# Moving where a one-core retention + feed-forward kernel rounds its weights, norms the next block and splits its output matrix

## The chip, the cores and the metric

The program runs on one core of one Trainium2 chip. The metric is the device time of one execution in microseconds (us), lower is better.

## The reference, cut to what matters

x has 4 sequences of 1024 tokens of width 512, in fp32. `LN` is a layer norm over the width without gain; lam is one decay for each of 16 heads.

```
h   = LN(x)
q, v = h @ Wq.T, h @ Wv.T                # 512 x 512 each
ret = scan over a sequence's tokens: state = lam * state + v_t
o   = LN(q * ret) * gamma + beta
o   = (o * silu(h @ Wg.T)) @ Wo.T
x   = x + LN(o)                           # "x1"
h   = LN(x)
g   = silu(h @ fp8(gate_w) * gate_scale)  # 512 x 1536, weights rounded to fp8 e4m3
u   = h @ fp8(up_w) * up_scale
d   = (g * u) @ fp8(down_w) * down_scale  # 1536 x 512
out = x + LN(d)
```

## The kernel before, in words

The 4096 tokens go through in 8 blocks of 512 (`NB = 8`), each with a retention part (class `Retention`) and a feed-forward part (class `Ffn`). The feed-forward part of block t runs in 12 steps (`for i in range(NI)`, one step for each 128 of the 1536 inner columns); between its products the order written out by hand places the retention part of block t+1, so that TensorE always has a product to run while the other engines do the element-wise work. In the loop `f` is the feed-forward part of block t, `b` is the retention part of block t+1, `n` that of block t+2 and `l` the feed-forward part before. Every engine takes its instructions in the order in which the program lists them (`InOrder`), so an instruction that waits holds up all that is listed behind it on its engine. SP issues nearly all transfers, in order too.

Ahead of the loop stands a long prologue. It runs block 0's retention part (`a`) with plain fp32 products, gets ready block 1's (`b`), and prepares weights for the whole run:

- **Roundings.** Gate, up and down weights come in 18 pieces of 1024 columns, in the order gate, up, down for each pair of steps (`pieces`). A piece is rounded by a VectorE cast to fp8 and a ScalarE activation back to fp32r (`round_weights`). One piece is three `yield`s, and `rounds(3)` runs one piece. Piece n is loaded into one of 7 buffers when an earlier piece has left it (`load_next`). Step i of block 0 needs the pieces of pair i//2; its down product runs two steps later (`lag = 2`).
- **Splits.** The q, v, g and o matrices are each split in four units into a top, a low and a scaled difference part (`Splitter.split`): three VectorE operations and one ScalarE activation. Units 0-3 are v, 4-7 q, 8-11 g, 12-15 o. `store` writes the parts to memory; later blocks stream them through a ring of four buffers (`w_ring`, `fetch_weights`). The units of o are loaded (`keep`), split and stored in block 1's steps; `Splitter.times` says when: `(block, step, place): "w12"` is a load, `s12` a split, `k12` a store, `r` new scratch room, `c12` a copy.
- **Block 1's x.** `b.stats`, `b.rstd`, `b.shift`, `b.norm_x` norm it (VectorE, GpSimd, ScalarE), `b.turn_x` transposes it on TensorE into banks pd0-pd3, `cut_x` takes the top part (VectorE, ScalarE) and the low part (VectorE), and `part_x` the difference. Then `b.begin(k, c)` runs the top and low passes of product k, unit c, ScalarE scales the bank, and `b.end(k, c)` adds the difference pass.
- **Block 1's norm of q * ret.** `halves` makes two fp32r halves of the sum (ScalarE, then VectorE), `mean` and `var` average them on TensorE, `center_y` subtracts and squares, `rstd_y` and `z` finish.

In step i of a block TensorE runs `f.gate(i)`, `f.up(i)` and `f.down(i - 2)`. Gate and up share two banks ("pf"): a gate product needs ScalarE's silu of the gate before (`gate<-pfg`), an up product needs VectorE's multiply of the up before (`gate<-pfu`). `fuse` then copies the result to fp32r on ScalarE and `rest` takes the remainder on VectorE. `scale(s)` takes the down sums from banks pd0-pd3 into `d`.

Down's weights in the kernel before lie in a changed order: of the 512 columns the even ones first and then the odd ones, written so by the rounding activation. `Ffn.down` reads them as `"p (k u) -> p u k"`, which gives the natural order in the bank. The same reading trick is used for fp32r products elsewhere; there the banks hold the two halves of a row in turns, and who reads such a bank does it through `in_order`.

Blocks 2-7 (`fast`) have no roundings, splits or prologue work.

Of the kernel before, what the change touches and what calls it, by code (L numbers as in the profile page):

```python
# [14 lines left out]
AF = mybir.ActivationFunctionType  # L15
ALU = mybir.AluOpType
# [7 lines left out]
def sandwich(  # L24
# [26 lines left out]
    NS = TB // P  # L51
# [15 lines left out]
    class InOrder:  # L67
# [42 lines left out]
    down_sb = wpool.tile([P, NI, D], F32R, tag="down_sb", name="down_sb")  # L110
    gate_v = gate_w.rearrange("(c p) f -> p c f", p=P)
    up_v = up_w.rearrange("(c p) f -> p c f", p=P)
    down_v = down_w.rearrange("(c p) f -> p c f", p=P)

    PW = 2 * NC * P
    pieces = []
    for h in range(NI // 2):
        pieces += [
            (gate_sb[:, :, ts(h, 2 * P)], gate_v[:, :, ts(h, 2 * P)]),
            (up_sb[:, :, ts(h, 2 * P)], up_v[:, :, ts(h, 2 * P)]),  # L120
            (
                down_sb[:, ts(h, 2), :].rearrange("p a (k u) -> p a u k", k=2),
                down_v[:, ts(h, 2), :],
            ),
        ]


# [10 lines left out]
    over = const.tile([P, len(pieces)], F32, tag="over", name="over")  # L138
# [28 lines left out]
    def as_dst(z, n):  # L167
        return z.rearrange("p (a b) -> p a b", a=2 if n % 3 == 2 else NC)

    def like(z, n):  # L170
        z = as_dst(z, n)
        return z.rearrange("p a (u k) -> p a u k", k=2) if n % 3 == 2 else z

    def load_piece(n):
        sp.dma_start(as_dst(parts[places[n]], n), pieces[n][1])

    def load_next(n):
        for m in range(n + 1, len(pieces)):
            if freed_by[m] == n:
                load_piece(m)  # L180

    def round_weights():


        for n in range(len(pieces)):
            w = parts[places[n]]
            if flag is None:
                yield
                act.copy(pieces[n][0], like(w, n))
                load_next(n)  # L190
                yield
            else:
                eighth = eighths[n % 2]
                dve.tensor_copy(eighth, w, saturate=False)
                load_next(n)
                yield
                act.activation(pieces[n][0], like(eighth, n), AF.Copy, accum_out=over[:, n : n + 1])
                yield
            yield

    rounding = round_weights()

    def rounds(n):
        for _ in range(n):
            next(rounding, None)
# [58 lines left out]
    def in_order(bank):  # L264

        return bank.rearrange("p (u k) -> p k u", k=2)
# [63 lines left out]
    class Splitter:  # L330
# [68 lines left out]
        def keep(self, n):  # L399
# [5 lines left out]

        times = {
            (0, 1, "end"): "c12", (0, 2, "end"): "c13", (0, 3, "end"): "c14", (0, 4, "end"): "c15",
            (1, 0, "mid"): "r w12 w13",
            (1, 0, "end"): "w14 w15", (1, 1, "end"): "s12", (1, 2, "start"): "s13",
            (1, 2, "end"): "k12 s14", (1, 3, "start"): "k13", (1, 3, "end"): "s15 k14",  # L410
            (1, 4, "mid"): "k15",
        }

        def at(self, *when):
# [491 lines left out]
    class Ffn:  # L906
# [60 lines left out]
        def scale(self, s):  # L967
            if s == 0:
                self.mv = small.tile([P, NS, 2], F32, tag="mv4", name=f"mvd_{self.t}", bufs=2)
            self.d[s] = work.tile([P, D], F32, tag="tok", name=f"d_{self.t}_{s}", bufs=4)  # L970
            dve.tensor_tensor(self.d[s], self.pds[s], ds_sb, ALU.mult)

        def stats(self, s):
            stats(self.d[s], self.mv[:, s, :])
# [49 lines left out]
    splitter = Splitter()  # L1024
    for n in range(8, 12):
        splitter.copy(n)
    b = Retention(1)
# [36 lines left out]
    a.scan(0)  # L1064
    a.v(1, "pf", later)
    a.scan(1)
    a.q(0)
    a.y_of(0)
    a.q(1)
    a.y_of(1)  # L1070
    splitter.split(8)
    a.v(2, "pf")
    a.scan(2)
    splitter.split(9)
# [2 lines left out]
    a.y_of(2)  # L1077
    splitter.split(10)
    splitter.store(9)
    b.stats(0)  # L1080
    a.v(3, "pf")
    a.scan(3)
    splitter.load("v")
# [2 lines left out]
    for n in range(4, 8):  # L1086
        splitter.copy(n)
    splitter.store(10)
    for s in range(1, NS):
        b.stats(s)  # L1090
    a.q(3)
    splitter.load("q")
    for n in range(4, 7):
        load_piece(n)
    a.y_of(3)
    b.rstd()
    b.shift()
    splitter.split(11)
    rounds(2)
    a.g_of(0, "pf")  # L1100
    for s in range(NS):
        b.norm_x(s, True)
    a.mean()
    a.center_y()
    splitter.store(11)
    b.new_xnT()
    a.g_of(1, "pf")
    b.turn_x(0, "pd0")
    b.turn_x(1, "pd1")
    b.cut_x(0)  # L1110
    b.cut_x(1)
    a.gate(2, "pf")
    b.turn_x(2, "pd2")
    b.turn_x(3, "pd3")
    b.cut_x(2)
    b.cut_x(3)
    splitter.split(0)
    rounds(3)
    a.silu(2)
    a.gate(3, "pf")  # L1120
    a.silu(3)
    splitter.store(0)
    a.var()
    for s in range(NS):
        b.part_x(s)
    a.rstd_y()
    for c, home in enumerate(("pa0", "pf", "pf", "pa1")):
        b.begin("g", c, home)
    for c in range(NC):
        a.z(c)  # L1130
    for c in range(NC):
        b.end("g", c)
    splitter.split(1)
# [1 line left out]
    a.o(0, "pd0")  # L1135
    splitter.split(2)
    splitter.store(1)
    rounds(3)
    a.o_moments(0)
    a.x1_of(0)  # L1140
    a.o(1, "pd1")
    splitter.split(3)
    splitter.store(2)
# [1 line left out]
    a.x1_moments(0)  # L1145
    a.x1_of(1)
    a.x1n_of(0)
    a.o(2, "pd2")
    rounds(1)
    a.o_moments(2)  # L1150
    a.x1_moments(1)
    a.x1_of(2)
    a.x1n_of(1)
    splitter.store(3)
    a.o(3, "pd3")
    splitter.split(4)
    a.new_x1nT()
    b.begin("v", 0, "pf")
    a.turn_x1n(0)
# [23 lines left out]
    splitter.store(5)  # L1183
    b.begin("q", 0, "pd2")
    b.end("v", 3)
    rounds(3)
    b.begin("q", 1, "pd3")
    a.turn_x1n(3)
    a.upper_of(3)
# [1 line left out]
    splitter.split(7)  # L1191
    splitter.store(6)
    a.rest_of(3)
    rounds(3)
    b.begin("q", 2, "pf")
    b.end("q", 1)
    b.begin("q", 3, "pf")
    rounds(3)
    b.end("q", 2)
    rounds(3)  # L1200
    b.end("q", 3)
    splitter.store(7)

    l = None
    for t in range(NB):
        f, n = Ffn(a), None
        fast = b is not None and b.fast
        for i in range(NI):
            if t > 0 and (t > 1 or i) and not (fast and i == 11):
                (f if i else l).rest((i - 1) % NI)  # L1210
            if t == 0 and i == 0:
                n = Retention(2)

            if t > 0 and b and i == 0 and t < NB - 2:
                n = Retention(t + 2)
# [23 lines left out]
            if t == 0 and 7 <= i < 11:  # L1239
                b.x1_moments(i - 7)  # L1240
            f.gate(i)
            if t == 0 and i in (4, 5):
                n.norm_x(2 * i - 8, True)
                n.norm_x(2 * i - 7, True)
            if fast and i < 7:
                b.gap(3 * i)
            if fast and 7 <= i < 10:
                b.o_gap(3 * i - 21)
            if t == 0 and i == 6:
                n.fetch_x()  # L1250
            splitter.at(t, i, "start")
            if n and t and i == 2:
# [27 lines left out]
            if t == 0 and i == 4:  # L1280
# [3 lines left out]
                b.z(3)  # L1284
            if t == 0 and 6 <= i < 10:
                b.o(i - 6)
            if t == 0 and i == 7:
                b.new_x1nT()
            if t == 0 and 7 <= i < 10:
                b.x1n_of(i - 7)  # L1290
# [81 lines left out]
            if n and t and i == 8:  # L1372
                n.low_of(2)
                n.low_of(3)
            if t == 0 and i in (7, 8):
                n.low_of(2 * i - 14)
                n.low_of(2 * i - 13)
            if t == 0 and i == 10:
                n.diff_of(0)
                n.diff_of(1)  # L1380
# [5 lines left out]
                    n.diff_of(2)  # L1386
                    n.diff_of(3)
            if t == 0:
                if i == 0:
                    rounds(3)  # L1390
                    b.halves()
                    rounds(3)
# [16 lines left out]
            if n and i == (6 if t else 5):  # L1409
                n.new_xnT()  # L1410
            if t == 0 and 6 <= i < 10:
                b.x1_of(i - 6)
# [72 lines left out]
        l, a, b = f, b, n  # L1485
# [116 lines left out]
```

## Time and profile before

| | |
|---|---|
| time, median of 3 runs (range) | 924.46 us (923.93 to 926.37) |
| the profiled execution | 924.62 us, its span 922.8 us |
| TensorE busy, instructions | 888.1 us (96%), 3948 |
| VectorE, ScalarE, GpSimd busy | 629.1 us, 424.7 us, 239.8 us |
| mean granted TensorE clock | 0.992 |

The span is from the first to the last instruction; the other 1.8 us of the profiled execution lie around it. In the profile every instruction of the kernel has line L75 (the helper `InOrder`), so groups are told apart by the names of their tiles: `pfg` and `pfu` are the banks of gate and up, `pd` of down, `pv`, `pq`, `pg` of the retention products, `ptx` of block 1's turned x, `mu` and `var` the averages, `scr` a buffer of raw weights, `split_room` the splits' scratch, `wo_parts` the split o. In a timeline the columns are start, duration, engine, operation, tiles and count; a bracket gives the idle time before it and what released it.

### The profile page before, as it was taken

How to read it: one execution, taken by the hardware profiler on the slowest of the kernel's cores; microseconds unless marked ns; L12 is line 12 of the kernel's file. 1: busy time of each engine (PE TensorE's matmuls, PEld its weight loads, DVE VectorE, ACT ScalarE, POOL GpSimd, SP SyncE). 2: the span in 40 equal slices, each digit the busy share in tenths (PEclk: the TensorE clock that was granted, in tenths of full speed). 3: DMA queues.
4: the chain of work that ended last, by engine and by line, in shares of the span. 5: the costliest groups of instructions: out<-in, count | busy, mean ns of one | idle time of the engine just before them, and what ended most of it. 6: DMA issues, size and time to landing. Idle time of an engine off the chain costs nothing. (4 is left out here: it accounts for less than half of the span.)

```text
span 922.8 us, 11982 instructions
## 1 busy us (share of the span) xinstructions
PE 888.1 (96%) x3948; PEld 742.6 (80%) x3948; DVE 629.1 (68%) x1071; ACT 424.7 (46%) x741; POOL 239.8 (26%) x304
## 2 busy tenths in 40 slices
PE   9999869999799999999999999999999999999995
PEld 7465657787688888888888888888888888888885
DVE  4878677658568775876758766686758755665545
ACT  1277666433354435553364534644364533644323
POOL 1214220311322314141232304232141502422030
PEclk9999999999899999999999999999999999999999
DMA  9963654557445666727745467537656365434021
GB/s 285 307 195 130 186 187 119 142 160 261 151 141 123 192 217 195 189 61 254 237 128 150 158 203 240 155 88 240 211 170 178 104 217 151 133 105 114 1 93 49
DMA packets 115579, 152.69 MB, mean 165 GB/s; under 512 B 10867, under 2 KB 54644, under 8 KB 115444
## 3 DMA queue, kind: packets, MB, share of 16 engines
q1 hardware_dynamic: 114644, 151.18, 53.3%
q10 hardware_dynamic: 864, 0.66, 0.3%
q8 instruction: 33, 0.54, 0.3%
q14 instruction: 38, 0.31, 0.1%
HBM read 117.46 MB, written 38.54 MB: 169 GB/s over the span
## 5 line engine op out<-in xcount | busy, mean ns | idle before, releaser
L75 PE MATMUL pfg<-x1nT,gate_sb 128*128 128x512 f32 x768 | 184.4, 383 | 2.1 <-ACT gate L75 1.9
L75 PE MATMUL pfu<-x1nT,up_sb 128*128 128x512 f32 x768 | 184.4, 383 | 0.7 <-DVE gate L75 0.7
L75 PE MATMUL pd<-down_sb,fuse 128*128 128x512 f32 x720 | 170.5, 379 | 0.0
L75 PEld LDWEIGHTS pfg<-x1nT,gate_sb 128*128 128x128 f32 x768 | 145.1, 190 | 26.0 <-ACT gate L75 5.1
L75 PEld LDWEIGHTS pfu<-x1nT,up_sb 128*128 128x128 f32 x768 | 146.1, 190 | 23.7 <-issue 1.4
L75 PEld LDWEIGHTS pd<-down_sb,fuse 128*128 128x128 f32 x720 | 141.3, 196 | 14.6
L75 DVE SCALAR_TENSOR_TENSOR gate<-pfu,us_sb,gate 128x512 f32<-128x512 f32 x96 | 71.8, 748 | 71.8 <-PE pfu L75 61.2
L75 ACT CAST fuse<-gate 128x512 fp32r<-128x512 f32 x90 | 55.6, 618 | 134.2 <-DVE gate L75 134.0
L75 ACT ACTIVATE gate<-pfg,gs_sb 128x512 f32<-128x512 f32 x96 | 65.7, 684 | 94.3 <-PE pfg L75 94.3
L75 POOL TENSOR_SCALAR mv<-mv 128x1 f32<-128x1 f32 (+1 forms) x82 | 22.2, 271 | 319.7 <-DVE mv L75 317.7
L75 DVE TENSOR_TENSOR fuse<-gate,fuse 128x512 fp32r<-128x512 f32 x90 | 70.5, 783 | 6.1 <-ACT fuse L75 6.1
L75 POOL TENSOR_TENSOR d<-d,x 128x512 f32<-128x512 f32 x28 | 41.7, 1511 | 86.0 <-ACT d L75 72.1
L75 DVE BATCH_NORM_STATS2 st<-x 128x6 f32<-128x512 f32 x64 | 43.5, 680 | 20.1 <-POOL x L75 17.3
L75 POOL TENSOR_TENSOR mv<-mv,nhalf 128x1 f32<-128x1 f32 (+1 forms) x75 | 52.7, 702 | 6.2
L75 POOL TENSOR_TENSOR x<-x,x1n 128x512 f32<-128x512 f32 x32 | 45.5, 1429 | 18.8 <-ACT x1n L75 11.8
L75 ACT ACTIVATE pv<-pv 128x512 f32<-128x512 f32 x28 | 16.3, 582 | 54.1 <-PE pv L75 54.1
L75 POOL TENSOR_TENSOR ysum<-y 128x512 f32<-128x512 f32 x8 | 10.8, 1347 | 108.6 <-DVE y L75 108.6
L75 POOL TENSOR_TENSOR sqsum<-sqsum,sq 128x512 f32<-128x512 f32 x24 | 33.4, 1390 | 17.3 <-ACT sq L75 15.5
L75 DVE TENSOR_TENSOR y<-pq,y 128x512 f32<-128x512 f32 x28 | 19.1, 681 | 23.0 <-PE pq L75 23.0
L75 DVE SCALAR_TENSOR_TENSOR y<-y,lnb_sb,mids 128x512 f32<-128x512 f32 x28 | 27.0, 965 | 7.1 <-ACT mids L75 7.0
L75 ACT ACT_TABLE_LOAD x19 | 24.4, 1283 | 16.0 <-DVE var L75 11.5
L75 DVE BATCH_NORM_STATS2 st<-po 128x6 f32<-128x512 f32 x32 | 21.9, 684 | 14.1 <-PE po L75 14.1
(214 smaller groups left out, 1494.0 us busy)
## 6 DMA issues: line engine op xcount, KB each, us to landing
x<-in_x SPq DMA_DIRECT2D x52, 256.0 KB, 5.2
kept<-x SPq DMA_DIRECT2D x32, 256.0 KB, 3.1
x<-kept SPq DMA_DIRECT2D x32, 256.0 KB, 4.2
out<-d SPq DMA_DIRECT2D x31, 256.0 KB, 2.0
w_ring<-dtop_v SPq DMA_DIRECT2D x24, 256.0 KB, 3.2
w_ring<-dlow_v SPq DMA_DIRECT2D x24, 256.0 KB, 3.7
w_ring<-ddiff_v SPq DMA_DIRECT2D x24, 256.0 KB, 3.7
w_ring<-dtop_q SPq DMA_DIRECT2D x24, 256.0 KB, 2.7
```

The costliest lines, as they stand in the source:

```text
L75: return lambda *args, **kwargs: tc.keep_in_program_order(op(*args, **kwargs))
```

## The change: what it does

Down's weights are rounded in their natural order, and `scale` reads the down banks through `in_order` instead. In the prologue block 1's `stats`, `norm_x`, `turn_x` and `cut_x` move from behind block 0's v, q products to between them; `silu(3)` moves behind `var` and `rstd_y`. The roundings of the prologue are spread anew (8 pieces before the loop as before), and in block 0's steps one piece is rounded in each of steps 0-5 and two in each of steps 6 and 7, where it was two in each of steps 0-4. Block 1's first `halves` moves to step 1 and its `mean` and `center_y` behind step 1's up product; its second `halves` goes before the roundings of step 2. Block 2's x is normed, sent, fetched and parted one step later in block 0 (stats in steps 0-3). Block 1's units of o are all loaded at the start of block 1's step 0, split in step 0 (two) and step 3 (two).

```diff
-            (
-                down_sb[:, ts(h, 2), :].rearrange("p a (k u) -> p a u k", k=2),
-                down_v[:, ts(h, 2), :],
-            ),
+            (down_sb[:, ts(h, 2), :], down_v[:, ts(h, 2), :]),
...
-                act.activation(pieces[n][0], like(eighth, n), AF.Copy, accum_out=over[:, n : n + 1])
+                act.activation(pieces[n][0], as_dst(eighth, n), AF.Copy, accum_out=over[:, n : n + 1])
...
-            (1, 0, "mid"): "r w12 w13",
-            (1, 0, "end"): "w14 w15", (1, 1, "end"): "s12", (1, 2, "start"): "s13",
-            (1, 2, "end"): "k12 s14", (1, 3, "start"): "k13", (1, 3, "end"): "s15 k14",
-            (1, 4, "mid"): "k15",
+            (1, 0, "start"): "r w12 w13 w14 w15", (1, 0, "mid"): "s12", (1, 0, "end"): "s13",
+            (1, 1, "start"): "k12", (1, 1, "mid"): "k13", (1, 3, "start"): "s14",
+            (1, 3, "end"): "s15", (1, 4, "start"): "k14", (1, 4, "end"): "k15",
...
-            dve.tensor_tensor(self.d[s], self.pds[s], ds_sb, ALU.mult)
+            halves = "p (k u) -> p k u"
+            dve.tensor_tensor(
+                self.d[s].rearrange(halves, k=2), in_order(self.pds[s]), ds_sb.rearrange(halves, k=2),
+                ALU.mult,
+            )
...
     a.scan(1)
+    b.stats(0)
     a.q(0)
     a.y_of(0)
+    b.stats(1)
+    b.stats(2)
     a.q(1)
     a.y_of(1)
+    b.stats(3)
+    b.rstd()
+    b.shift()
     splitter.split(8)
+    for s in range(NS):
+        b.norm_x(s, True)
     a.v(2, "pf")
...
-    b.stats(0)
+    b.new_xnT()
+    b.turn_x(0, "pd0")
+    b.turn_x(1, "pd1")
     a.v(3, "pf")
...
-    for s in range(1, NS):
-        b.stats(s)
+    b.turn_x(2, "pd2")
+    b.turn_x(3, "pd3")
+    b.cut_x(0)
     a.q(3)
...
-    b.rstd()
-    b.shift()
     splitter.split(11)
-    rounds(2)
+    b.cut_x(1)
     a.g_of(0, "pf")
-    for s in range(NS):
-        b.norm_x(s, True)
     a.mean()
     a.center_y()
     splitter.store(11)
-    b.new_xnT()
     a.g_of(1, "pf")
-    b.turn_x(0, "pd0")
-    b.turn_x(1, "pd1")
-    b.cut_x(0)
-    b.cut_x(1)
-    a.gate(2, "pf")
-    b.turn_x(2, "pd2")
-    b.turn_x(3, "pd3")
     b.cut_x(2)
     b.cut_x(3)
+    rounds(3)
+    a.g_of(2, "pf")
     splitter.split(0)
-    rounds(3)
-    a.silu(2)
     a.gate(3, "pf")
-    a.silu(3)
-    splitter.store(0)
     a.var()
     for s in range(NS):
         b.part_x(s)
     a.rstd_y()
+    a.silu(3)
+    splitter.store(0)
...
     for c in range(NC):
         a.z(c)
+    rounds(3)
     for c in range(NC):
         b.end("g", c)
...
     splitter.store(1)
-    rounds(3)
     a.o_moments(0)
     a.x1_of(0)
+    rounds(2)
     a.o(1, "pd1")
...
+    rounds(1)
     a.o(2, "pd2")
-    rounds(1)
+    rounds(3)
+    splitter.split(4)
     a.o_moments(2)
...
-            if t == 0 and i in (4, 5):
-                n.norm_x(2 * i - 8, True)
-                n.norm_x(2 * i - 7, True)
+            if t == 0 and i in (5, 6):
+                n.norm_x(2 * i - 10, True)
+                n.norm_x(2 * i - 9, True)
...
-            if t == 0 and i == 6:
+            if t == 0 and i == 7:
                 n.fetch_x()
...
             if t == 0 and i == 1:
-                b.mean()
-                b.center_y()
-            if t == 0 and i == 2:
-                n.stats(2)
-                n.stats(3)
-                n.rstd()
-                n.shift()
+                b.halves()
...
             f.fuse(i)
+            if t == 0 and i == 1:
+                b.mean()
+                b.center_y()
+            if t == 0 and i == 2:
+                b.halves()
...
-            if t == 0 and i in (7, 8):
-                n.low_of(2 * i - 14)
-                n.low_of(2 * i - 13)
+            if t == 0 and i in (8, 9):
+                n.low_of(2 * i - 16)
+                n.low_of(2 * i - 15)
...
             if t == 0:
-                if i == 0:
-                    rounds(3)
-                    b.halves()
-                    rounds(3)
-                elif i == 2:
-                    rounds(5)
-                    b.halves()
-                    rounds(1)
-                elif i < 6:
-                    rounds(6)
+                rounds(3 if i < 6 else 6 if i < 8 else 0)
                 if i < 11:
                     f.rest(i)
-                if i < 2:
+                if i < 4:
                     n.stats(i)
+                if i == 3:
+                    n.rstd()
+                    n.shift()
...
-            if t == 0 and i in (4, 5):
-                n.send_x(2 * i - 8)
-                n.send_x(2 * i - 7)
+            if t == 0 and i in (5, 6):
+                n.send_x(2 * i - 10)
+                n.send_x(2 * i - 9)
```

More of the change, by code (lines that the diff above doesn't have):

```diff
@@ L168, in as_dst @@
         return z.rearrange("p (a b) -> p a b", a=2 if n % 3 == 2 else NC)
-    def like(z, n):
-        z = as_dst(z, n)
-        return z.rearrange("p a (u k) -> p a u k", k=2) if n % 3 == 2 else z
     def load_piece(n):
@@ L188, in round_weights @@
                 yield
-                act.copy(pieces[n][0], like(w, n))
+                act.copy(pieces[n][0], as_dst(w, n))
                 load_next(n)
@@ L1155, in sandwich @@
     a.o(3, "pd3")
-    splitter.split(4)
     a.new_x1nT()
@@ L1193, in sandwich @@
     a.rest_of(3)
-    rounds(3)
     b.begin("q", 2, "pf")
     b.end("q", 1)
+    rounds(3)
     b.begin("q", 3, "pf")
-    rounds(3)
     b.end("q", 2)
@@ L1202, in sandwich @@
     splitter.store(7)
+    rounds(3)
     l = None
@@ L1286, in sandwich @@
                 b.o(i - 6)
-            if t == 0 and i == 7:
+            if t == 0 and i == 8:
                 b.new_x1nT()
@@ L1388, in sandwich @@
             if t == 0:
-                if i == 0:
-                    rounds(3)
-                    b.halves()
-                    rounds(3)
-                elif i == 2:
-                    rounds(5)
-                    b.halves()
-                    rounds(1)
-                elif i < 6:
-                    rounds(6)
+                rounds(3 if i < 6 else 6 if i < 8 else 0)
                 if i < 11:
                     f.rest(i)
-                if i < 2:
+                if i < 4:
                     n.stats(i)
+                if i == 3:
+                    n.rstd()
+                    n.shift()
             if l and not b and i in (4, 5):
@@ L1408, in sandwich @@
                     l.rstd()
-            if n and i == (6 if t else 5):
+            if n and i == 6:
                 n.new_xnT()
```

## The prediction

> **What bounds the kernel now.** I read the page first, then a table by stages, then TensorE's (PE's) timeline and the queues of ScalarE (ACT) and VectorE (DVE) around its gaps.
>
> ```profile
> span 922.8 us, 11982 instructions
> PE 888.1 (96%) x3948; PEld 742.6 (80%) x3948; DVE 629.1 (68%) x1071; ACT 424.7 (46%) x741; POOL 239.8 (26%) x304
> ```
> ```profile
> 109.00:150.00 41.00, 32.05 (x132) 25.53 (x132) 29.74 (x47) 29.60 (x44) 9.39 (x9) 0.96 0.51 172
> 232.00:262.00 30.00, 24.70 (x95) 20.12 (x96) 16.59 (x25) 11.72 (x21) 10.82 (x11) 0.89 0.46 149
> 300.00:900.00 600.00, 598.45 (x2776) 522.03 (x2775) 405.02 (x687) 269.31 (x471) 164.98 (x203) 1.00 0.53 161
> ```
>
> The columns of the stages are length, PE, weight loads, DVE, ACT, GpSimd (POOL), granted clock, DMA share, GB/s. From 300 to 900 us PE is busy 99.7% at clock 1.00: no reordering gains there, and the change leaves the products as they are. What can go lies before 262 us, where the same table (rows not shown) leaves PE idle 23.6 us. Its waits, with what a wait costs behind it:
>
> ```profile
> 106.85 1.99 PE L75 MATMUL pq<-up_sb,slot 128*128 128x512 f32 x8 [1.92 <-ACT pq L75]
> 116.55 0.49 PE L75 MATMUL mu<-half,mean_r 128*128 128x512 f32 x1 [2.26 <-ACT half L75]
> 127.37 1.99 PE L75 MATMUL pfg<-x1nT,gate_sb 128*128 128x512 f32 x8 [1.33 <-ACT gate L75]
> 132.84 0.50 PE L75 MATMUL var<-half,mean_r 128*128 128x512 f32 x1 [3.48 <-ACT half L75]
> 134.16 3.13 PE L75 MATMUL pfu<-x1nT,up_sb 128*128 128x512 f32 x8
> 232.70 2.07 PE L75 MATMUL pq<-diff,w_ring 128*128 128x512 f32 x4 [4.14 <-ACT pq L75]
> 248.07 0.49 PE L75 MATMUL mu<-half,mean_r 128*128 128x512 f32 x1 [3.31 <-ACT half L75]
> 249.13 3.45 PE L75 MATMUL pfg<-x1nT,gate_sb 128*128 128x512 f32 x8
> ```
>
> Eight fp32r matmuls take 1.73 us start to start elsewhere. After the three gaps over 3 us the next ones take 1.0 to 1.6 us more (clock 0.91 there); after 2.26 us they do not. The releasers are ACT and, behind them, DVE: queues with too much listed ahead of a short operation.
>
> ```profile
> 114.06 1.96 ACT L75 ACTIVATE down_sb<-scr 128x1024 fp32r<-128x1024 fp8e4 x1
> 115.89 0.60 ACT L75 CAST half<-ysum 128x512 fp32r<-128x512 f32 x1
> 117.86 1.06 ACT L75 ACTIVATE gate_sb<-scr 128x1024 fp32r<-128x1024 fp8e4 x1 [1.36 <-DVE scr L75]
> ```
>
> A down piece takes 2.0 us, a gate piece 1.06: the difference is down's changed order.
>
> I follow the new queues by hand with these durations: DVE cast, add or subtract 0.6-0.7, split 1.85, stats with aggregate 0.85; ACT gate, copy or scale 0.5-0.6, piece 1.25 with its accumulator read. Times are in the frame of before's timeline.
>
> **Down's order.** Six down pieces go from 2.04 to 1.06 us on ACT, 6 us in all, counted below only where PE waits. The price is a bank read at every second element in `scale`, 32 times, four of them in the tail where PE is done.
>
> ```profile
> L75 DVE TENSOR_TENSOR y<-pq,y 128x512 f32<-128x512 f32 x8 | 5.4, 680 | 5.4 <-PE pq L75 5.4
> L75 DVE TENSOR_TENSOR d<-pd,ds_sb 128x512 f32<-128x512 f32 x4 | 2.5, 677 | 0.0
> ```
>
> `y<-pq,y` already reads in this stride and takes 680 ns against 677 for the straight read: price nothing. The Trainium skill, page "SBUF — State Buffer", section "SBUF: two separate sides", speaks against the change: it puts PSUM in 8-byte lines and calls any non-contiguous access there significantly slower, at least for matmuls. Taken as a doubling, an estimate of mine, it would put the four reads in the tail and so the end 2.7 us later. The row shows no such price on DVE and decides.
>
> **Prologue to 68 us.** Block 1's x has all landed (at most 5.4 us after issue at 14.3) before its stats run. Four stats end at 26.2, GpSimd's chain (2.63 us, as at 41.55-44.18) behind its sum at 29.4, the norms on ACT (4 x 0.73) have the second x at 31.1; PE reaches the turn at 31.3. So the 1.11 us wait at 47.20 and its slow restart (0.3) go. New: silu(3) now stands behind the Sqrt load (var turned 56.3, loads 2 x 1.28, root 0.32, silu 0.6), ends at 59.8 and holds the bank that PE wants at 59.2: 0.75 in place of 0.25. o starts at 67.0 instead of 68.1: **1.1**. Bounds: 1.7 with no new wait; -0.9 if DVE's split is held up twice more, because a GpSimd operation beside its subtract makes it 1.64 instead of 0.69 us (as at 25.69).
>
> **To the loop, 68 to 109 us.** DVE goes without a break from the scan of v0 to split 6, 10.6 us (87.40-98.03), and still does: split 5, split 6, three scans. It starts 1.2 earlier, so PE's wait for q0's scale grows from 0.41 to 1.7 while the 0.91 before goes. The last q waits 1.2 instead of 1.92 (a down piece ahead of it on ACT, 1 us shorter). gate(0) starts at 106.5 instead of 108.83: **1.2** more. Bounds -1 and 3.2 (all three waits).
>
> **Steps 0-5 of block 0.** Before: gate(0) at 108.83, gate(6) at 150.24, 41.4 us. PE's work there is 16 x 1.73 for gates, ups and downs, 1.3 for mu and var, 28.9 in all; the rest is waits, slow clock and restarts. New waits: mu: gate(1)'s silu behind one piece (111.55 + 1.25) ends at 113.5, its halves at 114.1 and 114.9 while PE is there at 113.5: 1.5. gate(3): the squares, one piece and gate(2)'s silu end at 121.75, 0.85 late. var 0.6 in all, gates 4 and 5 about 0.2. With 5 restarts of 0.2: 28.9 + 3.15 + 1.0 = 33.1, so **8.3**. Block 2's first stats now stand ahead of half and multiply on DVE and wait for x issued at 108.3; I have it landed by 113, before it costs. Landing 8 us after issue (the slowest issues of the first 70 us) would cost 2.8. Bounds 4 and 12.5 (all waits).
>
> **Steps 6-11 of block 0.** Two pieces per step in 6 and 7 put 2.5 us on ACT ahead of block 1's o chain (stats, GpSimd, ACT, GpSimd add, stats, transpose), and block 2's `low_of` (2.2 us on DVE) moves to steps 8 and 9. Before PE never waited here; fuse(8) and fuse(9) now come 2-5 us late, covered by the o product (3.4) and down (1.7) between; fuse(10) comes at 181.5 with PE there at 180.6. Price **-1.0**, bounds 0 and -4.
>
> **Block 1.** Before, splits 13 and 14 stood in steps 2 and 3 ahead of multiplies that PE waited for.
>
> ```profile
> 227.66 1.64 DVE L75 TENSOR_TENSOR wo_parts<-wo_parts,split_room 128x512 fp32r<-128x512 f32 x1
> 230.77 0.74 DVE L75 SCALAR_TENSOR_TENSOR gate<-pfu,us_sb,gate 128x512 f32<-128x512 f32 x1
> 240.93 0.43 DVE L75 TENSOR_SCALAR split_room<-wo_parts 128x512 int32<-128x512 int32 x1 [4.54 <-DMA ddiff_o<-split_room]
> ```
>
> The last line is split 14 waiting for split 12's store, which now comes two steps earlier: that stall goes, and with it most of mu's wait; split 14 then costs 1.85 ahead of step 3's multiply, and mu's halves come 0.7 after PE. But splits 12 and 13 now stand ahead of the scans of v2 and v3 and wait for their loads: SP issues four from 203.5 on, DVE is there at 205.3 and goes on at 207.5 to 209. The scan of v3 then ends at 218.6-220, PE needs its bank at 218.9; the scale of q2 ends at 229.8-231.2 while PE is there at 228.4-229.8. And the ring's next load stands behind four more issues of 0.45 us. So 4.14 + 1.6 (slow clock) become 1.5 + 1.0: gain 3.2. At mu 3.31 becomes 0.7, gain 2.8 with the second half's 0.23; the slow clock behind it (1.6) goes too, but var then waits that much longer, for its chain hangs on mu: nothing. Together **6.0**, bounds 2 and 8.5.
>
> **Sum.** 1.1 + 1.2 + 8.3 - 1.0 + 6.0 = 15.6. The profiled execution took 924.62 (span 922.8 and 1.8 around it), 0.2 from the median: **909.0 us**. The ends of the terms will not all fall together; 905 to 913 for this case.
>
> **The rivals.**
> - *Given back* (917): the chain of block 1's o does not fit a step of 8.65 us; each of steps 8-11 loses 1.5 and block 1's scans start late. For it: fuse(8) some 5 us late by my own walk. Against: DVE was 64% busy from 150 to 200. 913 to 921.8.
> - *Everything goes* (900): the queues have more slack than my in-order walk gives, and 23.6 us of idle plus 4 of slow clock mostly vanish. Against: the two chains above are DVE-bound by rows. 896 to 905.
> - *Slower* (930): DVE becomes the bound from step 6 of block 0 to step 3 of block 1. Each of steps 6-11 takes 1.5-2 longer (10), the scans of v2 and v3 come 5 later behind two splits that wait for their loads, the halves and multiplies behind them as well, so the gaps over 3 us are back with their slow clock (11). It decides once a chain step takes over 11.5 us where 8.65 are to be had. Against: DVE's idle rows between 155 and 190 are waits of 1 to 3 us for PE and GpSimd, not a full queue.
> - *Nothing* (924): the waits only move by as much.
>
> **How the numbers follow.** This kernel can tell 0.3% (2.8 us) from no change. Chances: forecast 0.55, given back 0.19, everything 0.14, nothing 0.04, slower 0.08. Faster 0.88, same 0.04, slower 0.08. The range leaves out slower (0.08), nothing (0.04), the part of everything below 899 (0.04) and of given back above 920 (0.03): 899 to 920.
>
> **What would show it.** Right: down pieces at 1.06 us on ACT; no wait at the turn of block 1's x; gate(6) of block 0 near 139.5; waits for mu and var under 2 us in both blocks and no clock under 1.00 from 109 to 232; `d<-pd` still near 0.68 us. Wrong: PE waiting for `gate` or `x1nT` in steps 8-11, for `w_ring` or a scan in block 1's steps 0-2, or `st<-x` on DVE held by a DMA in step 0.

## The result, and the profile after

The changed kernel takes 912.7 us (median of 4 runs, 911.73 to 913.68) against 924.19 for the kernel before (4 runs, 923.03 to 926.37). The ratio is 0.9873, 95% interval 0.9851 to 0.9894: 11.7 us less (the medians differ by 11.5). The forecast was 909.0, 15.6 us less. The profiled execution took 913.0 us, its span is 911.2, and it is set against the profiled execution of before, 924.62 and 922.8.

The head of the page, and two stages (stretch, PE, weight loads, DVE, ACT, POOL, granted clock, DMA share, GB/s):

```profile
span 911.2 us, 11999 instructions
PE 884.0 (97%) x3948; PEld 741.0 (81%) x3948; DVE 631.3 (69%) x1071; ACT 419.0 (46%) x741; POOL 241.4 (26%) x304
```
```profile
109.00:150.00 41.00, 38.19 (x158) 30.43 (x157) 32.76 (x52) 25.33 (x42) 8.12 (x9) 0.96 0.49 166
150.00:200.00 50.00, 47.59 (x198) 36.98 (x197) 30.64 (x55) 22.55 (x46) 12.29 (x18) 1.00 0.59 171
```

From 109 to 150 us PE went from 32.05 to 38.19 us busy (158 matmuls instead of 132, for the changed kernel is further along by then), at the same mean clock of 0.96. From 150 to 200, where it never waited before, PE now stands idle 2.4 us. ACT lost 5.7 us of work in all: six down pieces shortened by 1.0 us. PE's timeline of the changed kernel shows which waits went and which came:

```profile
104.72 1.13 PE L75 MATMUL pq<-up_sb,slot 128*128 128x512 f32 x4 [0.81 <-ACT pq L75]
113.09 0.49 PE L75 MATMUL mu<-half,mean_r 128*128 128x512 f32 x1 [0.31 <-ACT half L75]
115.57 0.79 PE L75 MATMUL mu<-half,mean_r 128*128 128x512 f32 x1 [1.99 <-DVE half L75]
116.16 3.07 PE L75 MATMUL pfg<-x1nT,gate_sb 128*128 128x512 f32 x8
181.19 1.99 PE L75 MATMUL pfg<-x1nT,gate_sb 128*128 128x512 f32 x8 [1.53 <-ACT gate L75]
184.06 2.00 PE L75 MATMUL pfu<-x1nT,up_sb 128*128 128x512 f32 x8 [0.88 <-DVE gate L75]
204.14 1.13 PE L75 MATMUL pv<-low,w_ring 128*128 128x512 f32 x4 [2.10 <-DMA w_ring<-dlow_v]
214.02 1.13 PE L75 MATMUL pq<-diff,w_ring 128*128 128x512 f32 x4 [0.98 <-ACT pq L75]
248.19 1.52 PE L75 MATMUL var<-half,mean_r 128*128 128x512 f32 x2 [2.54 <-ACT half L75]
251.21 2.12 PE L75 MATMUL pfg<-x1nT,gate_sb 128*128 128x512 f32 x8
```

The four big waits of before (1.92 for the last q, 2.26 for mu, 3.48 for var, 4.14 for q2) are 0.81, 0.31, 0.29 and 0.47; block 1's mu is 0.90 in place of 3.31. New are DVE's half at 115.57, gate(11)'s wait for the silu of gate(10) at 181.19, the ring's load at 204.14, and a longer wait for block 1's var at 248.19 (0.83 before).

All runs are compared below by the starts of the same four products on PE: gate(0) and gate(6) of block 0, gate(0) and gate(7) of block 1. The columns are the lengths of the stretches between them, taken from each kernel's PE timeline.

| kernel | to gate(0) | steps 0-5 | steps 6-11 | block 1 to gate(7) | rest of the span |
|---|---|---|---|---|---|
| before | 108.83 | 41.41 | 49.67 | 77.16 | 645.7 |
| changed | 105.69 | 34.17 | 52.52 | 74.62 | 644.2 |
| e1 down alone | 107.88 | 40.02 | 49.57 | 77.53 | 646.0 |
| e2 prologue alone | 106.28 | 41.13 | 49.67 | 78.36 | 645.8 |
| e3 steps alone | 108.94 | 35.15 | 54.22 | 77.50 | 646.1 |
| e4 o's splits alone | 109.08 | 42.64 | 49.67 | 75.61 | 646.0 |
| f1 loads later | 105.70 | 33.01 | 52.52 | 75.07 | 647.1 |
| f2 stats later | 106.24 | 32.93 | 52.52 | 74.53 | 645.9 |
| f3 roundings earlier | 105.93 | 33.14 | 50.70 | 73.22 | 645.8 |
| f4 split 15 later | 105.51 | 34.90 | 52.51 | 70.72 | 646.7 |
| g1 old down order | 106.61 | 33.87 | 54.79 | 75.62 | 647.0 |
| g2 three edits | 106.00 | 32.92 | 51.08 | 70.10 | 646.4 |
| g3 five edits | 105.35 | 32.91 | 50.62 | 72.13 | 645.3 |
| h1 five and the loads | 106.10 | 32.94 | 50.75 | 72.29 | 647.2 |

One trace is one execution: e4's steps 0-5 have the instructions of before and took 1.2 us longer, at a clock of 0.89. The last column lies after all that the change moves, apart from the strided reads, and varies by 3 us among these kernels. So the 1.5 us that the changed kernel's trace has over before there are scatter, and only differences that a wait or a clock explains are read from single stretches. Across chips the ratios are compared.

### The profile page after: what moved, and what is told of

Its sections match the earlier page's. It is cut to its first block, busy times and chain, and to the rows that moved or that the text cites. A ratio compares the mean times of both kernels' runs of the same rounds, so it can differ in the third digit from the quotient of the medians.

```text
span 911.2 us, 11999 instructions
## 1 busy us (share of the span) xinstructions
PE 884.0 (97%) x3948; PEld 741.0 (81%) x3948; DVE 631.3 (69%) x1071; ACT 419.0 (46%) x741; POOL 241.4 (26%) x304
## 4 chain that ended last, share of the span: by engine, by line
PE 85%; DVE 7%; ACT 3%; DMA 2%; issue 1%; POOL 1%; DVEq 0%; SPq 0%; ACTq 0%; POOLq 0%
PE pfu L75 17%; PE pfg L75 16%; PE pd L75 15%; PE pg L75 9%; PE po L75 9%; PE pv L75 9%; PE pq L75 8%; DVE st L75 1%; DVE y L75 1%; PE idle L75 1%; DVE gate L75 1%; DMA x<-in_x 1%; PE var L75 1%; PE mu L75 1%; PE pt L75 1%
```

## The experiments

**The parts alone.** Each kernel is the kernel before with one part of the change, as the diff above has it.

*e1, down's order alone:*

```diff
-            (
-                down_sb[:, ts(h, 2), :].rearrange("p a (k u) -> p a u k", k=2),
-                down_v[:, ts(h, 2), :],
-            ),
+            (down_sb[:, ts(h, 2), :], down_v[:, ts(h, 2), :]),
```

> The kernel before with down's weights in natural order alone: six rounding pieces fall from 2.04 to 1.06 us on ACT, scale reads its bank in stride. My theory (the parts add, and a shorter piece counts only where PE waits behind it): of the pieces before the loop and in steps 0-4, those ahead of pq (1.92 at 106.85), mu (2.26 at 116.55) and var (3.48 at 132.84) matter, some 1 us each for two or three of them: 1 to 3 us less than before, about 922.5. Rival A (all in the ACT queue's length): the whole gain of the change comes from the shorter pieces, 6 us or more gone, 918 or less. Rival B (the strided reads cost): 32 reads dearer than 0.68 us, the same time as before or more, and the tail after 900 us longer.

Measured: ratio 0.9976 (0.9966 to 0.9987), 923.59 us against 925.02. The gain lies where a long piece stood ahead of PE: the last q's wait fell from 1.92 to 1.03, mu's from 2.26 to 1.49; var's rose from 3.48 to 4.32 and took some of it back. The reads of the down banks, first of before, then of the changed kernel (the tile's rows: count, min/median/max in ns, first and last start):

```profile
L75 DVE TENSOR_TENSOR d<-pd,ds_sb x32: 670/679/692, 224.2 to 914.2; 128x512 f32<-128x512 f32 x32
```
```profile
L75 DVE TENSOR_TENSOR d<-pd,ds_sb x32: 670/679/692, 218.8 to 902.5; 128x512 f32<-128x512 f32 x32
```

The strided read costs nothing (680 ns in e1), so rival B falls. So does rival A: 2.2 us, not 6. The theory's 1 to 3 us hold.

*e2, the prologue's order alone:* (the hunks from `a.scan(1)` to the loop)

```diff
+    b.new_xnT()
+    b.turn_x(0, "pd0")
+    b.turn_x(1, "pd1")
     a.v(3, "pf")
```

> The kernel before with the new order ahead of the loop alone (block 1's x normed and parted among block 0's products, the prologue's roundings spread anew; down still in the changed order, the loop as it was). Theory: the wait of 1.11 us at 47.20 and the slow restart go and gate(0) comes 2 to 3 us earlier than 108.83 (3.14 in the kernel after, some of it from shorter down pieces); nothing in the loop can take it back, since its queues start as much earlier: 921.5 to 922.5 in all. Rival (the wait moves): the wait for the ACT pieces ahead of the last q product grows by as much and gate(0) starts within 1 us of 108.83: 923.5 to 924.5.

Measured: ratio 0.9973 (0.9963 to 0.9983), 922.56 us. gate(0) starts at 106.28, 2.55 us earlier; the last q still waits 1.69. The theory's numbers hold.

*e3, block 0's steps alone:*

```diff
-                if i == 0:
-                    rounds(3)
-                    b.halves()
-                    rounds(3)
...
-                elif i < 6:
-                    rounds(6)
+                rounds(3 if i < 6 else 6 if i < 8 else 0)
```

> The kernel before with the new spread of roundings, halves, mean and block 2's x in block 0's steps alone (one piece in each of steps 0-5, two in 6 and 7; the prologue as it was; down pieces still 2.04 us). Theory: this is the largest term of the change: gate(0) to gate(6) took 41.4 us before and 34.2 after, so gate(6) comes some 5 to 7 us earlier, of which steps 6 to 11 give back 3 as they did in the kernel after (2.85): 3 to 4 us less in the end, about 920.5. Rival (the spread needs the short down pieces and the early prologue): pieces of 2.04 us in steps 2 and 5 hold silu and halves, gate(6) gains under 3 us and steps 6 to 11 give it all back: 923.5 or more.

Measured: ratio 0.9984 (0.9971 to 0.9996), 923.68 us. Steps 0-5 gain 6.3 us, as the theory said; then steps 6-11 give back 4.55, more than the 3 expected, and 1.5 us are left. What gave it back, in e3:

```profile
187.13 1.99 PE L75 MATMUL pfg<-x1nT,gate_sb 128*128 128x512 f32 x8 [2.43 <-ACT gate L75]
190.00 1.99 PE L75 MATMUL pfu<-x1nT,up_sb 128*128 128x512 f32 x8 [0.87 <-DVE gate L75]
```

So the theory had the gain of steps 0-5 right and the loss behind it too small. The rival, 923.5 or more, allows a gain of 0.7 us at most on the 924.19 above, and it looked for the loss in the wrong place (silu and halves in steps 2 and 5). The 1.5 us (0.4 to 2.7 by the interval) lie between the two.

*e4, o's splits alone:* (the table `times` of the change)

> The kernel before with o's splits in steps 0 and 3 of block 1 alone. Theory: the wait of 4.14 us at 232.70 and of 3.31 at 248.07 with their slow restarts (1.6 each) shrink, as in the kernel after, where block 1's steps 0-5 still held 2.10 for w_ring and 2.54 for var: gain 2.5 to 4, about 921. In the trace w_ring is waited for about 2 us behind the four loads of o. Rival (the splits' place does not matter, the wait only moves from step 2 to step 0 and from mu to var): within 1 us of before, 923.5 to 924.5.

Measured: ratio 0.9971 (0.996 to 0.9982), 922.57 us. Block 1's stretch gains 1.5 us in the trace and the runs 2.7: the q2 and mu waits shrank from 4.14 and 3.31 to 0.31 and 0.90, while 2.42 for dlow_v came and var rose to 2.54. The theory's lower end.

The four ratios add to 0.96% (8.9 us of 925); the whole change gives 1.27%, 2.9 us more. In the traces the parts fall short in two stretches: in steps 6-11, where alone they sum to -4.45 and the change has -2.85, and in block 1, where alone they sum to -0.36 and the change has 2.54. In block 1 part of it is the slow clock behind a wait: the gate behind the ring's late load took 2.76 us in e4 and 1.89 in the changed kernel, and the step with the wait of 4.14 us for q2 took 17.35 us in e2 and 16.20 before. This may be scatter; no run settles it. For steps 6-11 g1 below puts the question.

**The waits that were left.** Each kernel is the changed kernel with one edit.

*f1, two of o's loads later:*

```diff
-            (1, 0, "start"): "r w12 w13 w14 w15", (1, 0, "mid"): "s12", (1, 0, "end"): "s13",
-            (1, 1, "start"): "k12", (1, 1, "mid"): "k13", (1, 3, "start"): "s14",
+            (1, 0, "start"): "r w12 w13", (1, 0, "mid"): "s12", (1, 0, "end"): "s13",
+            (1, 1, "start"): "k12", (1, 1, "mid"): "k13 w14 w15", (1, 3, "start"): "s14",
```

> The changed kernel with two of o's four loads (w14, w15) moved from the start of block 1's step 0 to the middle of its step 1, behind the store of unit 13. Theory: the wait of 2.10 us for the ring's dlow_v at 204.14 is SP's queue (four loads issued from 196.35 on, dlow_v only at 198.51); with two issues fewer ahead of it the wait falls to about 1.2, and split 12's wait of 3.82 us for its load at 201.55 shrinks as well, since two transfers share the way instead of four. PE gains 0.9 there and perhaps 0.5 of the 0.98 for pq at 214.02: 911.5, 1 us less than the changed kernel's 912.7. Rival (the wait is swallowed): DVE's splits set the pace, pq at 214.02 waits by as much longer: 912.5 to 913.

Measured: ratio 0.988 (0.9864 to 0.9896), no gain over 0.9873. The ring's waits fell, and the wait for block 1's first q bank took their place. PE in f1:

```profile
201.92 1.13 PE L75 MATMUL pv<-low,w_ring 128*128 128x512 f32 x4 [0.63 <-DMA w_ring<-dlow_v]
213.09 1.68 PE L75 MATMUL pq<-diff,w_ring 128*128 128x512 f32 x4 [2.27 <-ACT pq L75]
```

The rival holds. ACT scales that bank in order behind the cast of `fuse`, which waits for DVE's multiply; and the multiply stands behind two splits, two scans and four stats (DVE's timeline has no gap from 200.62 to 211.9). Split 12 still waited 4.04 us for its load.

*f2, block 2's first stats one step later:*

```diff
-                if i < 4:
+                if i == 1:
+                    n.stats(0)
+                if 0 < i < 4:
                     n.stats(i)
```

> The changed kernel with block 2's first stats moved from the end of block 0's step 0 to the end of step 1. Theory: DVE stood idle 2.48 us at 114.03 for x, which was issued at 107.71, and the second half of block 1's q * ret stood behind it, so that PE waited 1.99 us at 115.57 and the clock fell to 0.96 (the gate product behind it took 3.07 us instead of 1.89). Without it mu's second wait is the usual 0.23 and the clock stays: 2 to 3 us less at gate(6), 910 to 911 in all. Rival (given back later): gate(6) comes 2 us earlier, but the o chain of steps 6 to 11 is as late as before and PE waits the more for the silu of gate(11): 912 to 913.

Measured: ratio 0.9851 (0.9836 to 0.9866) beside 0.9873: 2 us by the centres (910.4 on the scale of the 924.19 above, where the theory has it), not resolved by the intervals. The trace shows the wait that went. On DVE the changed kernel had

```profile
114.03 0.69 DVE L75 BATCH_NORM_STATS2 st<-x 128x6 f32<-128x512 f32 x1 [2.48 <-DMA x<-in_x]
```

and PE in f2

```profile
114.38 0.50 PE L75 MATMUL mu<-half,mean_r 128*128 128x512 f32 x1 [0.23 <-DVE half L75]
124.00 0.49 PE L75 MATMUL var<-half,mean_r 128*128 128x512 f32 x1 [1.37 <-ACT half L75]
```

The wait and the slow gate are gone (granted clock 1.00 from 109 to 150), and steps 0-5 take 32.93 instead of 34.17; of the 3 us that went, var takes back 1.1 behind two stats in step 1, and gate(3) 0.6. The gain depends on how late x lands: f1 and f3 have these stats where the changed kernel has them, x came earlier there, the second half waited 1.11 and 1.25 us instead of 1.99, and steps 0-5 took 33.01 and 33.14, as long as in f2.

*f3, roundings earlier:*

```diff
-                rounds(3 if i < 6 else 6 if i < 8 else 0)
+                rounds(3 if i < 4 or i in (6, 7) else 6 if i < 6 else 0)
```

> The changed kernel with one rounding piece in each of block 0's steps 0-3, two in 4 and 5, one in 6 and 7 (it was one in 0-5, two in 6 and 7). Theory: steps 6-11 gave 2.85 us back, because two pieces of 1.25 us in steps 6 and 7 each stand on ACT ahead of block 1's o chain; pfg at 181.19 waits 1.53 and pfu at 184.06 0.88. With one piece these go: 2 us less, 910.5 to 911.5, gate(6) unchanged to 0.5 later. Rival (the chain is late for DVE, not for ACT): fuse(8) and the silu of gate(11) wait for block 2's low_of and the stats of x1 on DVE; the waits stay within 0.5 us: 912.5 or more.

Measured: ratio 0.9854 (0.984 to 0.9869), again some 2 us by the centres, inside the theory's range. In f3 gate(11) no longer waits for the silu before it, and up(11) still waits for the multiply behind that silu:

```profile
178.71 1.89 PE L75 MATMUL pfg<-x1nT,gate_sb 128*128 128x512 f32 x8
181.46 2.00 PE L75 MATMUL pfu<-x1nT,up_sb 128*128 128x512 f32 x8 [0.86 <-DVE gate L75]
```

Steps 6-11 take 50.70 instead of 52.52, and steps 0-5 nothing more than f1's 33.01. So 1.8 of the 2.85 given back were the two pieces in steps 6 and 7. For the 0.86 on DVE the rival is right: there the multiply stands behind x1's stats.

*f4, o's last split later:*

```diff
-            (1, 3, "end"): "s15", (1, 4, "start"): "k14", (1, 4, "end"): "k15",
+            (1, 4, "start"): "k14", (1, 4, "mid"): "s15", (1, 4, "end"): "k15",
```

> The changed kernel with the split of o's last unit moved from the end of block 1's step 3 to the middle of its step 4. Theory: its three DVE operations (1.26, 1.65 and 1.65 us at 240.32 to 244.9) stand ahead of half of var's operand; PE's wait of 2.54 us for var at 248.19 and the slow clock behind it (1.5 us) go, less what the split costs in step 4: 2 to 3.5 us less, 909.5 to 911. Rival (it only changes place): the multiply and z of step 4 come 2 us later, PE waits at the o product or the next up instead: 912 to 913.

Measured: ratio 0.9823 (0.9809 to 0.9836), 4.6 us less than the changed kernel by the centres, more than the theory's 2 to 3.5, and the only single edit whose interval lies apart from 0.9873's. Split 15 on DVE, in the changed kernel and then in f4:

```profile
241.61 1.65 DVE L75 TENSOR_TENSOR wo_parts<-wo_parts,split_room 128x512 fp32r<-128x512 f32 x1
243.29 1.65 DVE L75 SCALAR_TENSOR_TENSOR split_room<-split_room,wo_parts 128x512 f32<-128x512 f32 x1
```
```profile
246.41 0.69 DVE L75 TENSOR_TENSOR wo_parts<-wo_parts,split_room 128x512 fp32r<-128x512 f32 x1
247.13 0.69 DVE L75 SCALAR_TENSOR_TENSOR split_room<-split_room,wo_parts 128x512 f32<-128x512 f32 x1
```

What lay beside it in the changed kernel, on POOL:

```profile
240.01 4.38 POOL L75 TENSOR_TENSOR sqsum<-sqsum,sq 128x512 f32<-128x512 f32 x3
```

The third operation, the first in order, took 1.26 and 0.42. A split is 1.8 us on DVE, and 4.6 beside POOL's sums of squares; POOL's three sums took 4.38 and 4.33. The Trainium skill, page "SBUF — State Buffer", section "Who interferes with whom", says that a VectorE instruction with two inputs in SBUF contends with a GpSimd instruction that reads SBUF, and that the one that comes second is blocked outright rather than slowed. The two operations with two inputs agree in that each stands about 0.96 us longer; whether it was blocked or slowed these rows do not tell. Nor is it this split alone: in f4 a subtract of step 3, `rest`, with two inputs in SBUF, lies beside the same sums and takes 1.52 instead of 0.68 us, while the multiply behind it, which reads a bank, takes 0.75 as elsewhere. In f4 PE goes through var without a wait:

```profile
240.64 1.52 DVE L75 TENSOR_TENSOR fuse<-gate,fuse 128x512 fp32r<-128x512 f32 x1
245.81 0.77 PE L75 MATMUL var<-half,mean_r 128*128 128x512 f32 x2
```

The granted clock stays at 1.00 from 200 to 262 us, and block 1's stretch takes 70.72 us instead of 74.62.

**Down's order within the whole.** *g1, the changed kernel with down in the old order* (the first hunk of the diff and `scale` turned back):

> The changed kernel with down's weights back in the changed order (pieces of 2.04 us on ACT, straight read in scale). The four parts alone gained 2.4, 2.5, 1.3 and 2.5 us, 8.7 together, the whole change 11.7; so 3 us come from parts together. Theory: they come from down and the new spread of roundings, since two pieces stand in each of steps 6 and 7 and one in 2 and 5: with long pieces the spread alone gave back 4.5 us in steps 6-11, the whole change 2.85. Taking natural order away then costs more than its 2.2 us alone: 4 to 5.5 us, 916.5 to 918, with the silu of gate(11) waited for 2.4 us or more instead of 1.5. Rival (the parts with shared waits are prologue and steps, down is worth the same everywhere): 2 to 2.5 us slower, 914.5 to 915.3.

Measured: ratio 0.9911 (0.9894 to 0.9927), 0.38% above the changed kernel's, with intervals that just meet; 3.5 us, between the theory's 4 to 5.5 and the rival's 2 to 2.5. The trace tells where. PE in g1:

```profile
183.54 3.52 PE L75 MATMUL pfg<-x1nT,gate_sb 128*128 128x512 f32 x8 [2.43 <-ACT gate L75]
```

Steps 6-11 take 54.79 against 52.52: the natural order is worth 2.3 us there once two pieces stand in steps 6 and 7, and on the kernel before nothing (e1's trace is 0.1 us shorter there). That is one place where the parts do not add. By the ratios the natural order is worth 3.5 us within the whole and 2.2 alone, which is 1.3 of the 2.9 us; the intervals are wider than that, and the rest stays open.

**Together.** *g2, the edits of f2, f3 and f4:*

> The changed kernel with three single edits together: block 2's first stats in step 1, two pieces in steps 4 and 5 instead of 6 and 7, o's last split in step 4. Theory: the three waits lie in three separate stretches, so the gains add: 1.2 (from gate(0) to gate(6)), 1.8 (from gate(6) to block 1's gate(0)) and 3.9 (block 1's steps 3-5) as the traces have them, 6.9 less than the changed kernel's 912.7: 905.5 to 907. Rival (an earlier gain is lost at a later wait, as with the loads): 908.5 or more, with a new wait over 1.5 us in block 1.

Measured: ratio 0.9813 (0.9794 to 0.9831), 908.24 us against 925.97. By the stretches up to block 1's gate(7) it stands 6.9 us ahead of the changed kernel (260.10 against 267.00), as the theory has it; by the ratios 0.60%, 5.5 us. On the scale of the 924.19 above it is 906.9, inside the theory's range, though the interval reaches the rival. The longest wait left in block 1 is 1.70 for the ring.

*g3, stats one per step as well, and splits 12 and 13 one place later:*

```diff
-            (1, 0, "start"): "r w12 w13 w14 w15", (1, 0, "mid"): "s12", (1, 0, "end"): "s13",
-            (1, 1, "start"): "k12", (1, 1, "mid"): "k13", (1, 3, "start"): "s14",
+            (1, 0, "start"): "r w12 w13 w14 w15", (1, 0, "end"): "s12",
+            (1, 1, "start"): "k12 s13", (1, 1, "mid"): "k13", (1, 3, "start"): "s14",
...
-                if i == 1:
-                    n.stats(0)
                 if 0 < i < 4:
-                    n.stats(i)
+                    n.stats(i - 1)
                 if i == 3:
+                    n.stats(3)
```

> The kernel of three edits, with block 2's stats one per step (0 in step 1, 1 in step 2, 2 and 3 in step 3) and o's splits 12 and 13 one place later (end of step 0, start of step 1). Theory: with two stats in step 1 var waited 1.37 us at 124.00, and with one it is 0.58 or less; a split that waits 3.8 us for its load on DVE no longer stands ahead of the scan of v2, so pq's wait near 214 (0.98) goes: 1.5 to 2 us less than the three edits, 904 to 905. Rival (SP's queue sets block 1's steps 0-1, not DVE's): the wait for the ring's dlow_v of 2.1 us stays and the scans only change places with the splits: the same as the three edits to 0.7 us.

Measured: ratio 0.9799 (0.9785 to 0.9814), 908.1 us: 1.3 us less than g2 by the centres, between the rival's 0.7 and the theory's 1.5, and not resolved by the intervals. The trace has both: the waits that the theory named went, and the ring's stayed, as the rival said. var waits 0.57 and the first q bank 0.23, but the ring's load comes 2.70 late and the gate behind it runs slowly, so that block 1's stretch takes 2 us longer than g2's. PE in g3:

```profile
201.24 1.13 PE L75 MATMUL pv<-low,w_ring 128*128 128x512 f32 x4 [2.70 <-DMA w_ring<-dlow_v]
202.21 3.15 PE L75 MATMUL pfg<-x1nT,gate_sb 128*128 128x512 f32 x8
```

*h1, g3 with the loads of f1:*

> The kernel of five edits (the three, stats one per step, splits 12 and 13 one place later) with two of o's four loads moved from block 1's step 0 to step 1 as well. The kernel of five edits still waited 2.70 us for the ring's dlow_v at 201.24, and the gate behind it took 3.15 instead of 1.89 us. Theory: the loads gained nothing alone because DVE's splits stood ahead of the scans (pq then waited 2.27); with the splits behind the scans that wait is 0.23, so the shorter ring wait now counts: 2.70 becomes 0.8 as in the run of the loads alone and the slow gate goes, 2 to 3 us less than 0.9799 of before, 0.977 to 0.978. Rival (block 1's steps 0 and 1 are bound by the transfers as a whole, whatever their order): another wait for the ring or for a split's load of 2 us appears at the later loads, 0.979 to 0.981.

Measured: ratio 0.9808 (0.9788 to 0.9828), 909.14 us: no gain, and the theory is wrong. PE no longer waits for the ring, nor for a later load, so the rival's reason is wrong too. The wait went to the first q bank again:

```profile
211.14 1.78 PE L75 MATMUL pq<-diff,w_ring 128*128 128x512 f32 x4 [2.65 <-ACT pq L75]
```

g3's 0.23 at that place was small because PE came there late itself. The bank came free about a microsecond earlier than in g3 (211.14 against 212.05 and f1's 213.09), but PE came earlier still. What sets it is ACT's queue: split 13's activation (209.32), the `fuse` cast and then the scale, all behind DVE's split 13 and multiply (207.42 to 209.95). A version that moves split 13 behind that multiply was not run.

The best two, g2 and g3, are 0.981 and 0.980 of before, against 0.987 for the change.

## Why the prediction was right or wrong

The direction and the mechanism were right: the time went from waits on ACT's and DVE's queues before 262 us, and the range (899 to 920) holds 912.7. By its terms:

- **Down's order, nothing on DVE**: right, 679 ns strided and straight. The section of the Trainium skill that the prediction weighed (page "SBUF — State Buffer", section "SBUF: two separate sides") speaks of matmuls; for this VectorE read no run here shows the price. Pieces fell to 1.06-1.07 us as said.
- **To gate(0), 1.1 + 1.2**: 3.14 came, 0.3 of which is the start of the first product. Right for the prologue: o starts 1.5 earlier, `pg` waits 0.96 where 0.75 was said. Too cautious behind it: the two q waits are 0.58 and 0.81 where 1.7 and 1.2 were said. e2 gives 2.55 without the short pieces.
- **Steps 0-5, 8.3**: 7.24 in the changed kernel's trace, but 8.4 and 8.3 in f1 and f3, which have the same code as far as mu and var. The difference is x for block 2, which the prediction put at 113 "before it costs"; DVE had it at 113.2 to 114.4 in the traces of the changed kernel, f1, f3 and f4, and stood 1.6 to 3.0 us for it. Its own price for a late x (2.8) is what f2 took away (2.9 before its own new waits). The mechanism was named and its chance set too low.
- **Steps 6-11, -1.0**: -2.85. The step that failed is the size: fuse(10) was said to be 0.9 late, and the silu that gate(11) waits for came 1.53 late and the multiply behind it another 0.88. f3 shows that the pieces on ACT are 1.8 of it.
- **Block 1, 6.0**: 2.54, the largest miss, and it has two steps. For the splits 3.2 was said; gate(0) to gate(3) went from 36.92 to 35.44, so 1.48. The text named the ring's load behind four issues but gave it no price, and it waited 2.10. At mu 2.8 was said and 2.40 came (gate(3) to gate(4), 12.30 to 9.90). For var it said "nothing", as the wait grows by what the slow clock saves; the wait did (0.83 to 2.54), but PE then ran slowly behind it, 1.1 us lost from gate(4) to gate(5). What it overlooked is why var is late: split 15 at 4.6 us beside POOL, which the prediction had priced elsewhere (1.64 instead of 0.69) and did not look for here. The trace of before already had it, hidden behind a PE that was late itself:

```profile
253.00 1.65 DVE L75 TENSOR_TENSOR wo_parts<-wo_parts,split_room 128x512 fp32r<-128x512 f32 x1
```

  With f4's edit the stretch gains 6.4.

The sum, before rounding: 3.14 + 7.24 - 2.85 + 2.54 = 10.07, and 1.5 in a stretch that no term covers and that varies as much without the change. That this one trace comes near the 11.7 of the ratio is in part chance: with the 8.3 of f3 in steps 0-5 the terms would give 11.1. Of the signs that the prediction set for itself, four came (down pieces at 1.06 us, no wait at the turn of block 1's x, gate(6) at 139.86, `d<-pd` at 0.68) and two did not: var of block 1 waits 2.54 us, and the clock is 0.96 from 109 to 150 us. All three signs of being wrong came as well: the waits for `gate` in step 11, for `w_ring` in block 1's step 0, and `st<-x` held by a DMA. The time still fell because these waits are shorter than those that went. Of the rivals *given back* was partly right, with its place (the o chain of block 1) and half its size, so that a value between it and the forecast came. *Slower* had the splits waiting for their loads right: split 12 stood 3.82 us for its load. PE paid little for that: 0.98 at the first q bank. Its 2.10 for the ring was for a load issued behind the same four loads of o, not for the splits.

## What to carry to other kernels

When queues run in order, price every wait that a moved instruction can bring, and above all the ones that you can name: three terms fell short here by 6.4 us together, and 2.8 of that lie where two hazards had no price, the ring's load, which the text named, and split 15 beside GpSimd, whose row stood in the trace. Look at the duration of an operation where it stands, not only in its group's mean: the same split is 1.8 or 4.6 us depending on what GpSimd does beside it, and moving it by one place was worth more than any single part of the change. A small wait says little of the slack behind it, since it depends on how late the waiting engine came: compare the times at which the awaited thing is done.

## What the runs showed of the hardware

- TensorE's clock fell after shorter gaps than the prediction had it ("gaps over 3 us"), and not each time. A gap of 2.54 us ahead of var was followed by a slow stretch in the changed kernel (the four `pg` products behind var took 1.91 us instead of 1.03, the gate behind them 2.12 instead of 1.89), and one of 2.53 at the same place in f1 was not:

```profile
248.82 0.50 PE L75 MATMUL var<-half,mean_r 128*128 128x512 f32 x1 [2.53 <-ACT half L75]
250.75 1.89 PE L75 MATMUL pfg<-x1nT,gate_sb 128*128 128x512 f32 x8
```

  A gap of 1.99 us, 0.5 us of work behind one of 0.31, cost 1.2 us on the gate at 116.16. The same gap of 4.14 us ahead of q2 was followed by a longer slow stretch in e2 than before (step 2 of block 1 took 17.35 and 16.20 us). The Trainium skill, page "TensorE: Matmul & The Clock Gate", section "What's actually happening", gives an idle window of about 3.4 us that runs free of the kernel's start. That it runs free would fit the two outcomes of one gap, which no run tests further; that it takes 3.4 us of idling does not fit these rows, and the measurement decides.
- The same loads of x, issued at 107.5 to 108.0 us in four kernels with the same order (the changed kernel, f1, f3 and f4), landed 5.4 to 6.9 us after issue, and the stretch varied by 1.9 us with it (33.01 to 34.90). So a wait for a transfer in one trace is one draw of several.
